# Queries and keys of two heads as one product on two levels of Strassen's algorithm, with the sums of tokens kept in DRAM

## The chip, the core and the metric

The kernel runs on one core of a Trainium2 chip. A core has five engines that run side by side and meet only at semaphores: TensorE (PE) multiplies matrices into the eight banks of PSUM, VectorE (DVE), ScalarE (ACT) and GpSimd (POOL) do elementwise work, and SyncE (SP) issues transfers to 16 DMA engines. [...] The metric is the time of one execution on the device in microseconds (us); lower is better.

## What is computed

One transformer block on 1024 tokens of width 512 in f32: layer norm, causal attention with 32 heads of width 128, its output projection added to the input, then a second layer norm and a network of three layers with weights of plus and minus one. Cut to what the change touches:

```python
q = einsum('bsd,de->bse', hidden_states, wq).reshape(B, S, H, DQ)   # DQ = 192, the first 128 are used
kv = einsum('bsd,de->bse', hidden_states, wkv)
k = kv[..., :H * DN].reshape(B, S, H, DN)
v = kv[..., H * DN:H * (DN + DV)].reshape(B, S, H, DV)
scores = einsum('bqhd,bkhd->bhqk', q[..., :DN], k) * DQ ** (-0.5)
probs = softmax(where(causal, scores, -1e30))
attn = einsum('bhqk,bkhd->bqhd', probs, v).reshape(B, S, H * DV)
return einsum('bse,ed->bsd', attn, wo)
```

## The kernel before

**Tiles and pairs.** The normalised tokens stand transposed in SBUF as `xnT` (128 partitions, 4 chunks of the width, 1024 tokens; L245). Heads are worked on in 16 pairs (`G` = 2). Each pair has 16 steps, one for each head and block of 128 queries. While a pair's scores, softmax and values run, the queries and keys of the next pair are made.

**One level of Strassen's algorithm.** A product of a 2 x 2 and a 2 x 2 arrangement of blocks takes eight block products, or seven if sums of blocks are multiplied. `products(which, g)` (L356) makes the queries (`which` = 0), keys (1) or values (2) of a pair with seven. The two halves of the width are the inner index, the two heads one outer index, the two halves of the tokens the other. The sums of tokens `T` are made once (`token_sums`, L285), the sums of weights for each pair on POOL (`weight_sums`, L307). For queries and keys, each of the seven products is two matmuls of 512 columns; for values, eight of 128. Products go into three PSUM banks, named X, Y and Z, and each `yield` ends one of the seven. X takes products 1 and 3, Y takes 2, 4 and 6, Z takes 5 and 7; a bank is read out (by ACT into `p1`, by DVE in `plus`) before the next product is accumulated into it. Pair 0 has plain products (`qk_plain`, L321).

**Scores and softmax.** `probabilities` (L513) multiplies queries and keys into `sc`, a single tile of two banks; DVE applies the mask and finds the extreme (L528), ACT takes the exponential and scales (L539, L544). `transpose_blocks` (L547) transposes 32 x 32 blocks on DVE, and `exchange` (L585) moves these blocks to where the transposed matrix has them, with 16 DMAs for each 512 queries. `attend` (L598) multiplies with the values some steps later.

**Order.** Matmuls and the transfers of `load` (L64) are pinned: they run on TensorE and SP in the order in which the program emits them. Other instructions are ordered by a scheduler. What TensorE does in a step is chosen by a planner in the loop from L700. Each step first emits the next step's scores and softmax (L750). After steps 3, 7, 11 and 15 it emits an `exchange` (L754). Then it takes products from the chain of 21 (7 for the values of this pair, 7 for the queries and 7 for the keys of the next) and parts of the output projection, up to a goal of columns (L761). The attend falls four steps after its exchange for the first 512 queries and six for the second (`ATTEND_AFTER`, L661). Weights are loaded at steps 2, 7, 12 and 15.

Of the kernel before, what the change touches and what calls it, by code (L numbers as in the profile page):

```python
# [19 lines left out]
G = 2  # L20
# [9 lines left out]
def kernel(  # L30
# [55 lines left out]
    heads = pool("heads", 4)  # L86
# [5 lines left out]
    ps_mm = pool("ps_mm", 3, space=bass.MemoryType.PSUM)  # L92

    DH = D // 2

    w_raw, w_sum, wv_sb, wo_sb = {}, {}, {}, {}
# [5 lines left out]
    def load_qk_weights(which, g, heads_of=range(G)):  # L102
        if (which, g) not in w_raw:
            w_raw[which, g] = pairs.tile(
                [P, G, NC, DN], F32, tag="wraw", name=f"w{'qk'[which]}{g}"
            )
        for i in heads_of:
            h = g * G + i
            if which == 0:
                src = wq_v[:, :, h, :DN]  # L110
            else:
                src = wkv_v[:, :, h * DN : (h + 1) * DN]
            load(w_raw[which, g][:, i, :, :], src)
# [21 lines left out]
    zeros = const.tile([P, P], F32, tag="zeros", name="zeros")  # L135
    nc.vector.memset(zeros, 0.0)
    idle = ps_sc.tile([P, S], F32, tag="sc", name="ps_idle")
    for _ in range(13):
        nc.tensor.matmul(idle[:, :P], lhsT=zeros, rhs=zeros, start=True, stop=True)  # L139
# [12 lines left out]
        fill=BIG,  # L152
# [124 lines left out]

# [13 lines left out]
    def A(which, g, i, j):  # L291
        c = slice(2 * j, 2 * j + 2)
        if which == 2:
            return wv_sb[g][:, c, i * DV : (i + 1) * DV]
        return w_raw[which, g][:, i, c, :]
# [11 lines left out]
    def weight_sums(which, g):  # L307
        w_sum[which, g] = sums_of(
            lambda i, j: A(which, g, i, j), "wsum", f"wsum{'qkv'[which]}{g}", 2
        )  # L310

    qT, kT, vs, attn = {}, {}, {}, {}

    def new_qk(which, h):
        dst = (qT, kT)[which]
        dst[h] = heads.tile(
            [P, S], F32, tag=("qT", "kT")[which], name=f"{'qk'[which]}T{h}", bufs=(4, 3)[which]
        )
        return dst[h]

    def qk_plain(between):  # L321
# [3 lines left out]
        for which, h in outs:  # L325
            new_qk(which, h)
        banks = {}
        for n_units in range(NT * 2 * G):
# [8 lines left out]
            for c in range(NC):  # L337
                matmul(
                    banks[n][:, i * P : (i + 1) * P],
                    lhsT=w_raw[which, 0][:, h, c, :],  # L340
                    rhs=xnT[:, c, t * P : (t + 1) * P],
                    start=(c == 0),
                    stop=(c == NC - 1),
                    skip_group_check=True,
                )
            if i == TPB - 1:
                keep_first(
                    nc.scalar.activation(
                        (qT, kT)[which][h][:, k * QB : (k + 1) * QB],
                        banks[n],  # L350
                        AF.Copy,
                        scale=(-scale, 1.0)[which],
                    )
                )

    def products(which, g):  # L356


        s = w_sum[which, g]
        mul = (-scale, 1.0, 1.0)[which]  # L360
        n = f"{'qkv'[which]}{g}"
        if which == 2:
            d = []
            for h in (g * G, g * G + 1):
                vs[h] = heads.tile([P, NT, DV], F32, tag="v", name=f"v{h}", bufs=3)
                d.append([vs[h][:, k * TPB : (k + 1) * TPB, :] for k in range(NQB)])
        else:
            d = [
                [t[:, k * QB : (k + 1) * QB] for k in range(NQB)]
                for t in (new_qk(which, g * G), new_qk(which, g * G + 1))  # L370
            ]

        def bank(name):
            shape = [P, TPB, DV] if which == 2 else [P, QB]
            return ps_st.tile(shape, F32, tag="st", name=f"{name}_{n}")

        def kept(name):
            shape = [P, TPB, DV] if which == 2 else [P, QB]
            return const.tile(shape, F32, tag=name, name=f"{name}_{n}")

        def product(ps, a, b, first, last):
            for c in range(2):
                start, stop = first and c == 0, last and c == 1
                if which != 2:
                    matmul(
                        ps,
                        lhsT=a[:, c, :],
                        rhs=b[:, c, :],
                        start=start,
                        stop=stop,  # L390
                        skip_group_check=True,
                    )
                    continue
# [10 lines left out]
        def plus(out, ps, other):  # L404
            if which == 0:
                nc.vector.scalar_tensor_tensor(out, ps, mul, other, ALU.mult, ALU.add)
            else:
                nc.vector.tensor_tensor(out, ps, other, ALU.add)

        X = bank("X")  # L410
        product(X, A(which, g, 0, 0), B(0, 0), True, False)
        p1 = kept("p1")
        nc.scalar.activation(p1, X, AF.Copy, scale=mul)
# [4 lines left out]
        plus(u2, Y, p1)  # L418
        yield
        product(X, A(which, g, 0, 1), B(1, 0), False, True)  # L420
        nc.scalar.activation(d[0][0], X, AF.Copy, scale=mul)
# [3 lines left out]
        plus(u3, Y, p1)  # L425
# [3 lines left out]
        plus(d[1][1], Z, u3)  # L429
        yield  # L430
        product(Y, A(which, g, 1, 1), T[3], False, True)
        plus(d[1][0], Y, p1)
        yield
        product(Z, s[3], B(1, 1), False, True)
        plus(d[0][1], Z, u2)
# [77 lines left out]
    def probabilities(h, qt):  # L513
        n = (qt + 1) * P
        sc = ps_sc.tile([P, S], F32, tag="sc", name=f"sc{h}_{qt}")
        for first in range(0, n, QB):
# [3 lines left out]
                lhsT=qT[h][:, qt * P : (qt + 1) * P],  # L520
                rhs=kT[h][:, cols],
# [10 lines left out]
            scale=1.0,  # L532
# [25 lines left out]
    def transpose_last(qt, p):  # L558
        qb, i = divmod(qt, TPB)
        if i == 0:  # L560
            spare = (heads, "qT"), (heads, "qT"), (heads, "kT"), (heads, "v")
            bufs = {"kT": 3, "v": 3}
# [3 lines left out]
            else:  # L566
                last_pT[qb] = [
                    pl.tile(
                        [P, 2, TPB, P], F32, tag=tag, name=f"pT_last{m}", bufs=bufs.get(tag)
                    )  # L570
                    for m, (pl, tag) in enumerate(spare)
                ]
        for m in range(qt // 2 + 1):
# [24 lines left out]
    def attend(h, qb, pT):  # L598
        g, j = divmod(h, G)
# [6 lines left out]
        if h == H - 1:  # L606
            ps = ps_mm.tile([P, TPB, P], F32, tag="mm", name=f"ps_av{h}_{qb}")
            for kc in range(nk):
# [7 lines left out]
                )  # L616
            nc.vector.tensor_copy(dst.rearrange("p (t i) -> p t i", t=TPB), ps)
            return
        ps = ps_mm.tile([P, NB, TPB, B32], F32, tag="mm", name=f"ps_av{h}_{qb}")
        for kc in range(nk):  # L620
# [7 lines left out]
            )  # L628
        nc.vector.tensor_copy(dst.rearrange("p (t a i) -> p a t i", a=NB, i=B32), ps)  # L629
# [3 lines left out]
    def products_of_pair(g):  # L633
        yield from products(2, g)
        if g + 1 < NG:
            yield from products(0, g + 1)
            yield from products(1, g + 1)
# [14 lines left out]


    def score_cols(qt):
        return (qt + 1) / TPB

    def value_cols(qb):
        return qb * TPB + (TPB + 1) / 2

    PRODUCT, O_PART = 2.0, 1.0  # L660
    ATTEND_AFTER = (TPB, TPB + 2)  # L661
# [35 lines left out]
    weight_sums(2, 0)  # L697
    load_qk_weights(0, 1)

    for i, (h, qt) in enumerate(steps):  # L700
# [3 lines left out]
        if s == 0:  # L704
            n_chain = 21 if g + 1 < NG else 7
# [3 lines left out]
            if g + 2 < NG:  # L709
                out_by = [max(0, (14 * (t - 2) + 12) // 13) for t in range(G * NT)]  # L710
            elif g + 2 == NG:
                out_by = [0, 0, 0, 2, 4, 6, 6, 8, 10, 12, 13, 14, 14, 14, 14, 14]
            else:
                out_by = [max(0, t - NT + 1) for t in range(G * NT)]
            done, chain_done, out_done = 0.0, 0, 0
            total = (
                2 * G * sum(score_cols(t) for t in range(NT))
                + PRODUCT * n_chain
                + o_cols * n_out
            )  # L720
            chain_end = 14 if g + 1 < NG else 6
        if s == 0:
            chain = products_of_pair(g)
            if g + 1 < NG:
                weight_sums(0, g + 1)
        if h == 2 and qt == 0:
            ffn_constants()
        if s == 2:
            if g + 1 < NG:
                load_qk_weights(1, g + 1)  # L730
# [4 lines left out]
        if s == 6 and g + 1 < NG:  # L735
            weight_sums(1, g + 1)
# [5 lines left out]
        if s == 12:  # L742
            if g + 1 < NG:
                weight_sums(2, g + 1)
            if g + 2 < NG:
                load_qk_weights(0, g + 2)
# [10 lines left out]
        late = i not in to_attend  # L757
        if not late:
            done += value_cols(to_attend[i][1])
        goal = total * (s + 1) / (G * NT)  # L760
        while True:  # L761
            want_chain = chain_done < min(n_chain, n_chain * (s + 1) / chain_end)
            want_out = out_done < min(n_out, out_by[s])
            if want_chain and (done < goal or chain_done + 2 < n_chain * (s + 1) / chain_end):
                next(chain)
                chain_done += 1
                done += PRODUCT
            elif want_out and (done < goal or out_done + 2 < out_by[s] or g + 2 == NG):
                next(o_chain)
# [4 lines left out]
            if not late:  # L774
                attend(*to_attend.pop(i))
                late = True
        if not late:
            attend(*to_attend.pop(i))
# [5 lines left out]
        if h == H - 1:  # L784
            if qt == 0:
                attend(h, 1, None)
# [31 lines left out]
    h1[1] = (part(keep, "pT0", "h1_hi1"), part(pairs, "wraw", "h1_lo1", 2))  # L818

    def network_input(t):  # L820

        k, i = divmod(t, TPB)
        pl, tag = ((heads, "kT"), (work, "p"))[k] if i < 3 or k == 1 else (heads, "v")
        xn = pl.tile([P, D], F32, tag=tag, name=f"xn_f{t}", bufs=3)
# [73 lines left out]
    attend(H - 1, 0, None)  # L898
# [12 lines left out]
    h1[0] = (part(keep, "tb0", "h1_hi0"), part(heads, "qT", "h1_lo0", 2))  # L911
# [44 lines left out]
```

## Time and profile before

Three runs took 1355.72 to 1356.49 us, median 1355.75. The profiled execution took 1356.68 us; its span from first to last instruction is 1354.9 us.

| group of instructions | count | busy us | mean ns |
|---|---|---|---|
| TensorE, scores, all widths | 768 | 290.1 | 486 |
| TensorE, probabilities by values | 744 | 250.3 | 486 |
| TensorE, first products of queries (X_q), 512 columns | 120 | 56.4 | 592 |
| DVE, sum out of PSUM for keys (u_k), 512 wide | 30 | 20.7 | 691 |
| ACT, copy out of PSUM for keys (p_k), 512 wide | 15 | 8.7 | 581 |
| POOL, sums of value weights, first of four, 256 wide | 16 | 11.7 | 728 |
| POOL, sum for the output (L457), 512 wide | 14 | 17.8 | 1269 |
| DMA, exchange of blocks, 128 KB and 64 KB | 992 | – | – |

A matmul of f32 stands in the trace as two records. Records overlap, since matmuls are pipelined, so a mean of 592 ns is the stay of one record and not its price; the price is read from the distance between starts. The DMA queue of SP moved 138.22 MB, with the 16 DMA engines busy 48.6% of the time; half the exchange's issues are of 128 KB and half of 64 KB. The granted clock of TensorE shows as 9 (90% or more) in all 40 slices.

### The profile page before, as it was taken

To read this page: it belongs to the slowest core of one execution; us is meant where nothing else is said; L and a number is where in the kernel's file an instruction comes from. 1 tells how busy PE (TensorE), PEld (TensorE's weight loads), DVE (VectorE), ACT (ScalarE), POOL (GpSimd) and SP (SyncE) were. 2 spreads that over 40 slices of the span, in tenths; PEclk is the share of its full clock that TensorE was granted. 3 is DMA by queue.
4 is the path that set the end of the run, shared out by engine and by line. 5 is a ranking of instruction groups with operands and counts; after the bars stand their busy time and mean duration, and the time that the engine had idled before them with its cause. 6 is when DMAs were issued, how large, how long until landed. Compare 5 with 4: busy or idle time off the path is not lost.

```text
span 1354.9 us, 16376 instructions
## 1 busy us (share of the span) xinstructions
PE 1346.6 (99%) x5598; PEld 873.1 (64%) x5598; DVE 806.8 (60%) x1669; ACT 500.0 (37%) x928; POOL 262.6 (19%) x324
## 2 busy tenths in 40 slices
PE   9999999999999999999999999999999999999999
PEld 9747575665757566575756657575665756657567
DVE  5455565656556565665656566565656656676574
ACT  3534333333333333343333334333333333335331
POOL 3311122211212221121222102122120212110200
PEclk9999999999999999999999999999999999999999
DMA  5356464444646444564644456464455545446301
GB/s 187 78 109 125 90 133 90 103 96 97 140 88 129 96 91 99 106 140 82 130 95 88 104 109 139 79 126 94 88 113 109 125 87 117 88 82 129 66 1 63
DMA packets 259651, 139.27 MB, mean 103 GB/s; under 512 B 18288, under 2 KB 253552, under 8 KB 259568
## 3 DMA queue, kind: packets, MB, share of 16 engines
q1 hardware_dynamic: 259568, 138.22, 48.6%
q8 instruction: 45, 0.74, 0.2%
q14 instruction: 38, 0.31, 0.1%
HBM read 38.54 MB, written 2.10 MB: 30 GB/s over the span
## 4 chain that ended last, share of the span: by engine, by line
PE 99%; DVE 1%; ACT 0%; issue 0%; ACTq 0%; DVEq 0%
PE sc L79 18%; PE ps_av L79 18%; PE ps_o L79 15%; PE Y_v L79 6%; PE Y_k L79 6%; PE Y_q L79 6%; PE Z_v L79 4%; PE X_v L79 4%; PE X_q L79 4%; PE Z_q L79 4%; PE Z_k L79 4%; PE X_k L79 4%; PE ps_qk L79 2%; PE ps_h L79 2%; PE ps_out L79 1%; PE ps_idle L139 0%
## 5 line engine op out<-in xcount | busy, mean ns | idle before, releaser
L539 ACT ACTIVATE p<-p,nmax 128x128 f32<-128x128 f32 (+7 forms) x256 | 199.0, 777 | 674.3 <-DVE nmax L528 672.3
L79 PE MATMUL sc<-kT,qT 128*128 128x512 f32 (+3 forms) x768 | 290.1, 486 | 1.4 <-DVE nmax L528 1.4
L79 PE MATMUL ps_av<-pT,v 128*128 128x512 f32 x744 | 250.3, 486 | 0.0
L528 DVE CUSTOM_DVE_ANT_0 p<-sc,mask 128x128 f32<-128x128 f32 (+7 forms) x256 | 191.3, 747 | 90.4 <-PE sc L79 90.4
L550 DVE STREAM_TRANSPOSE tb<-p 128x128 f32<-128x128 f32 (+1 forms) x248 | 187.2, 769 | 75.8 <-ACT p L544 72.2
L544 ACT ACTIVATE p<-p,rtotal 128x128 f32<-128x128 f32 (+7 forms) x256 | 197.0, 775 | 78.1 <-DVE rtotal L543 78.0
L79 PEld LDWEIGHTS ps_av<-pT,v 128*128 128x128 f32 x744 | 141.0, 190 | 127.7 <-issue 103.1
L79 PEld LDWEIGHTS sc<-kT,qT 128*128 128x128 f32 x768 | 138.7, 190 | 90.0 <-issue 77.5
L491 DVE TENSOR_TENSOR acc<-acc,ps_o 128x512 f32<-128x512 f32 x190 | 128.7, 682 | 56.0 <-PE ps_o L79 50.8
L79 PE MATMUL ps_o<-wo,attn 128*128 128x256 f32 (+1 forms) x400 | 111.3, 414 | 0.3 <-DVE attn L629 0.3
L543 DVE RECIPROCAL rtotal<-total 128x1 f32<-128x1 f32 x256 | 40.3, 158 | 113.2 <-ACT p L539 112.9
L79 PEld LDWEIGHTS ps_o<-wo,attn 128*128 128x128 f32 x400 | 72.9, 190 | 30.6 <-issue 22.3
L452 POOL TENSOR_TENSOR at<-attn,attn 128x512 f32<-128x512 f32 x14 | 17.7, 1262 | 348.3 <-DVE attn L629 348.3
L629 DVE COPY attn<-ps_av 128x512 f32<-128x512 f32 x62 | 42.2, 680 | 49.8 <-PE ps_av L79 49.8
L79 PEld LDWEIGHTS X_v<-wv,xnT 128*128 128x128 f32 x512 | 62.2, 192 | 5.1
L79 PE MATMUL X_v<-wv,xnT 128*128 128x128 f32 x512 | 62.3, 275 | 0.0
L79 PEld LDWEIGHTS ps_o<-osum,at 128*128 128x128 f32 x224 | 42.5, 190 | 22.8 <-issue 19.1
L301 POOL TENSOR_TENSOR wsumk<-wk 128x256 f32<-128x256 f32 x15 | 10.9, 726 | 235.6 <-PE Z_v L79 124.7
L79 PE MATMUL X_q<-xnT,wq 128*128 128x512 f32 x120 | 56.4, 592 | 0.0
L79 PE MATMUL X_k<-xnT,wk 128*128 128x512 f32 x120 | 56.4, 592 | 0.0
L79 PE MATMUL ps_o<-osum,at 128*128 128x256 f32 x224 | 55.0, 379 | 0.0
L539 ACT ACTIVATION_READ_ACCUMULATOR p<-p,nmax 128x1 f32 x256 | 48.1, 188 | 0.0
(177 smaller groups left out, 1648.6 us busy)
## 6 DMA issues: line engine op xcount, KB each, us to landing
pT<-tb SPq DMA_DIRECT2D x496, 128.0 KB, 3.1
pT<-tb SPq DMA_DIRECT2D x496, 64.0 KB, 2.1
wq<-in_L_attn_wq_dram SPq DMA_DIRECT2D x32, 256.0 KB, 3.3
wk<-in_L_attn_wkv_dram SPq DMA_DIRECT2D x32, 256.0 KB, 4.2
wv<-in_L_attn_wkv_dram SPq DMA_DIRECT2D x16, 512.0 KB, 4.0
wo<-in_L_attn_wo_dram SPq DMA_DIRECT2D x16, 512.0 KB, 3.7
x_in<-_attn_hidden_states_dram SPq DMA_DIRECT2D x8, 256.0 KB, 5.4
acc<-_attn_hidden_states_dram SPq DMA_DIRECT2D x8, 256.0 KB, 7.1
```

The costliest lines, as they stand in the source:

```text
L79: keep_order(nc.tensor.matmul(*args, **kw))
L301: nc.gpsimd.tensor_tensor(t[:, 0], a(1, 0), a(1, 1), ALU.add)
L452: nc.gpsimd.tensor_tensor(t0, b(0, 1), b(0, 0), ALU.subtract)
L491: nc.vector.tensor_tensor(dst, dst, ps, ALU.add)
L528: nc.vector.tensor_tensor_reduce(out=p[:, :n], in0=sc[:, :n], in1=mask[:, S - n :], scale=1.0, scalar=BIG, op0=ALU.add, op1=ALU.min, accum ...
L539: nc.scalar.activation(p[:, :n], p[:, :n], AF.Exp, bias=nmax, scale=-1.0, accum_out=total)
L543: nc.vector.reciprocal(rtotal, total)
L544: nc.scalar.activation(p[:, :n], p[:, :n], AF.Copy, scale=rtotal)
L550: nc.vector.transpose(tb[qb][:, : qt + 1, :, i, :], p[:, :n].rearrange("p (c b k) -> p c b k", b=NB, k=B32))
L629: nc.vector.tensor_copy(dst.rearrange("p (t a i) -> p a t i", a=NB, i=B32), ps)
```

## The change

Queries and keys of both heads of a pair become one product on two levels. The outer level has as its inner index the halves of the width, and as outer indices queries or keys and the halves of the tokens. Each of its seven products is again done with seven, over the halves within the half width, the two heads, and quarters of the tokens. That makes 49 matmuls of 256 columns where there were 2 x 7 x 2 = 28 of 512. Two outer products that go to the same outputs share a bank, side by side, so the 49 are worked through in four groups: three with two outer products (seven units of two matmuls each) and a last one with a single outer product (seven units of one matmul).

- The weights of a pair stand in one tile `w_qk` of seven slots; POOL makes the outer sums in place (`qk_weight_sums`) and the inner sums group by group (`qk_block_sums`).
- The inner sums of tokens are the same for every pair. They are made once in pair 0 (`make_t`, steps 1, 2, 4 and 5), stored in DRAM, and read back for each group of each pair into four single buffers t0 to t3 (`load_t`). A load for the next group is emitted right after the product that used the buffer.
- Outputs are accumulated in SBUF: groups 0 and 1 write their parts, POOL combines halves of them, groups 2 and 3 add theirs (`add_to` on POOL, `plus` on DVE).
- The planner: products carry a first and a due step. Groups 0 to 2 of the next pair run in steps 7 to 14, group 3 in steps 0 to 2 of that pair beside the value products. Attends are emitted in parts of two matmul chunks and interleaved with products. The output projection's due steps and the weights' loading steps move.
- The scale is applied in DVE's first softmax operation and the mask's sign is turned. Queries and keys of a head share a tile. There are 10 warm-up matmuls instead of 13.

```diff
+    HB = QB // 2
+    GROUPS = (
+        ((0, B(0, 0)), (5, T[1])),
+        ((2, T[2]), (4, T[0])),
+        ((1, B(1, 0)), (3, T[3])),
+        ((6, B(1, 1)),),
+    )
...
+    def make_t(grp):
+
+        bs = [b for _, b in GROUPS[grp]]
+        t = [new_t(n, f"new{grp}") for n in range(4)]
+        for m, b in enumerate(bs):
+            r = [x[:, m] for x in t]
+            nc.gpsimd.tensor_tensor(r[0], right(b, 0, 1), right(b, 0, 0), ALU.subtract)
+            nc.gpsimd.tensor_tensor(r[1], right(b, 1, 1), r[0], ALU.subtract)
+            nc.gpsimd.tensor_tensor(r[3], right(b, 1, 0), r[1], ALU.subtract)
+            nc.gpsimd.tensor_tensor(r[2], right(b, 1, 1), right(b, 0, 1), ALU.subtract)
+        for n in range(4):
+            t_kept[grp, n] = dram.tile(
+                [P, len(bs), HB], F32, tag=f"t{grp}{n}", name=f"t_kept{grp}{n}"
+            )
+            load(t_kept[grp, n], t[n][:, : len(bs)])
...
+    def load_t(grp, n, g):
+        t_now[n] = new_t(n, f"{grp}_{g}")
+        nm = len(GROUPS[grp])
+        load(t_now[n][:, :nm], t_kept[grp, n])
...
+        def product(ps, a, b, first, last):
+            for m in range(nm):
+                matmul(
+                    ps[:, m],
+                    lhsT=a[:, m, :],
+                    rhs=right(bs[m], *b) if isinstance(b, tuple) else t_now[b][:, m],
...
+            if not isinstance(b, tuple) and (nxt or g + 1 < NG):
+                load_t(nxt, b, g + (nxt == 0))
...
+        X = bank("X")
+        product(X, a00, (0, 0), True, False)
...
+        product(Y, s1, 1, True, False)
+        u2 = kept("u2")
+        plus(u2, Y, p1)
+        add_to(u2, 0, 1)
+        yield
+        product(X, a01, (1, 0), False, True)
...
+        product(Y, s2, 2, False, False)
+        u3 = kept("u3")
+        plus(u3, Y, p1)
+        add_to(p1, 1, 0)
+        add_to(u3, 1, 1)
+        yield
...
+        product(Z, s0, 0, True, False)
...
+        product(Y, a11, 3, False, True)
...
+        product(Z, s3, (1, 1), False, True)
...
+        for to, add in {0: ((1, 0),), 1: ((2, 1), (1, 3), (3, 2))}.get(grp, ()):
+            for h in hs:
+                d = qk[h].rearrange("p w (m n) -> p (w m) n", m=2)
+                nc.gpsimd.tensor_tensor(d[:, to], d[:, to], d[:, add], ALU.add)
+        if grp < 2:
+            qk_block_sums(grp + 2, g)
...
+        chain = [[2.0, 0, n, values] for n in range(7)]
+        if g > 0:
+            last = qk_products(3, g)
+            for at, step in ((0, 0), (2, 0), (3, 0), (5, 1), (6, 1), (8, 2), (9, 2)):
+                chain.insert(at, [0.5, 0, step, last])
         if g + 1 < NG:
...
+            first, n = NT - 1, 0
+            for grp in range(3):
+                gen = qk_products(grp, g + 1)
+                for _ in range(7):
+                    n += 1
+                    chain.append([1.0, first, first + (n * NT - 1) // 21, gen])
...
+        if g == 0 and s in (1, 2, 4, 5):
+            make_t((1, 2, 4, 5).index(s))
+            if s == 5:
+                for n in range(4):
+                    load_t(0, n, 1)
+        if g + 1 < NG:
+            if s == 3:
+                qk_weight_sums()
+            if s in (4, 5):
+                qk_block_sums(s - 4, g + 1)
...
         if qt % TPB == TPB - 1 and h < H - 1:
             qb = qt // TPB
             to_attend[i + ATTEND_AFTER[qb]] = (h, qb, exchange(h, qb))
...
+        if s == G * NT - 1 and g + 2 < NG:
+            for which in range(2):
+                load_qk_weights(which, g + 2)
...
+            if chain and chain[0][1] <= s and (
+                chain[0][2] <= s or done < goal and chain[0][2] <= s + 1
+            ):
+                cols, _, _, gen = chain.pop(0)
+                mine.append(gen)
+                done += cols
```

## The prediction

> **What bounds the kernel now.** I read the busy table first, then the chain of waits, then the chain's pieces in order of time through one pair of heads, then the timelines of the DMA queue and of POOL.
>
> ```profile
> PE 1346.6 (99%) x5598; PEld 873.1 (64%) x5598; DVE 806.8 (60%) x1669; ACT 500.0 (37%) x928; POOL 262.6 (19%) x324
> PE 99%; DVE 1%; ACT 0%; issue 0%; ACTq 0%; DVEq 0%
> ```
>
> TensorE has no idle time worth naming, and the chain that ended last is TensorE from end to end. Removed TensorE work is therefore worth its full time, and an added wait costs its full time: nothing absorbs it. The pieces (start, length, what) give the price of each unit:
>
> ```profile
> 600.39 1.72 PE X_q L79 x4
> 602.11 0.86 PE ps_o L79 x4
> 612.65 1.72 PE sc L79 x4
> 661.91 1.78 PE X_v L79 x16
> ```
>
> A matmul of f32 is two records. A 512-column matmul takes 0.86 us (1.72 for two), a 256-column one 0.432 us (0.86 for two ps_o), so half the columns cost half the time. One pair lasts 680.02 - 600.39 = 79.6 us (from one X_q to the next).
>
> **TensorE work removed.** Before: 14 products x 1.717 = 24.04 us per pair for queries and keys. After: 49 matmuls of 256 columns x 0.4325 = 21.19 us. Saved 2.85 us x 15 pairs = **-42.7 us**. The weight loads (190 ns, two per matmul) stay beside the matmuls, as they do for ps_o.
>
> **Work added on the other engines, per pair.** DVE: sums out of PSUM grow from 10 of 512 columns to 16 of 512 (0.69 us each, as u_k) and 6 of 256 (about 0.42, as the 256-wide copy of pT_last): +6.7 us on some 50. ACT: +0.9 us. POOL: its 512-element sum takes 1.27 us (the at row), its 256-element sum 0.73. Weight sums 4 x 1.27, block sums 12 x 0.73 and 4 x 0.42 (an estimate from those two), values 4 x 0.73, additions into u2, p1, u3 3 x 1.27 and 3 x 0.73, combinations of halves 8 x 1.27: 34.6 us where 8.8 us stood; with the sums for the output POOL works 43 of 77 us. None becomes the bound; TensorE's 77 us hide them where a product has time until its bank is wanted. That time shrinks: the next product into the same bank comes one product later, which was 1.72 us and is now 0.865, while one DVE sum takes 0.69 plus the hand-over. Following the planner's loop for a middle pair, four places have such neighbours (steps 8, 10, 12, 14), and the first scores of the next pair follow the last product directly. Each costs nothing if DVE is free and about 1 us if a 1 us softmax operation stands ahead. Step 8 is hidden by the wait found below; for the rest I take 0.7 us a pair, 14 pairs: **+10 us** (ends 0 and 42, at 3 us a pair, if POOL's additions into group 2 are late for step 14). The mask's sign, the scale moved into DVE's first operation and the scale dropped from ACT change no count: 0. Three fewer warm-up matmuls: 0, since the first rows are ready at about 5.8 us and the clock is not up before 7 us anyway.
>
> **The loads of token sums.** Each pair adds 16 loads (12 of 256 KB, 4 of 128 KB). Their bytes are no trouble (DMA 49% busy); their place in SP's queue is. Each buffer t0 to t3 is single, so a load can go out only after the product that read it, and SP issues in program order. Group 0's products start in step 7, and in step 7 the 16 DMAs of `exchange` are put into the queue before any product. So the loads of group 1 stand behind this:
>
> ```profile
> 619.78 11.10 SPq L66 DMA_DIRECT2D pT<-tb  x16
> wq<-in_L_attn_wq_dram SPq DMA_DIRECT2D x32, 256.0 KB, 3.3
> ```
>
> The exchange starts at 619.78, when the transpose for the 1024-column scores (piece at 612.65) is done: 7.1 us after these scores start. It holds SP for 11.1 us. A 256 KB load then lands 3.3 us after issue, taken from the weights, the nearest row (the output's 256 KB take 2.0, its ends 2.0 to 4.2). So the first load of group 1 lands 7.1 + 11.1 + 3.3 = 21.5 us after those scores start. TensorE wants it as group 1's second product, and counted by the planner there lie between: scores 1.72, last value product 1.78, scores 0.22, group 0's seven products 6.06, half an attend 2.16, scores 0.43, one output unit 0.86, scores 0.65, group 1's first product 0.86: 14.7 us. **TensorE waits 6.8 us in each of 14 pairs: +95 us** (ends 5.5 and 8). Behind the waiting matmul, in pinned order, stands everything TensorE does: the next scores, so DVE and ACT too. The other three loads of group 1 go out right after and land in time; group 2's are emitted before step 11's exchange, group 3's and the next group 0's have more than 10 us to spare.
>
> Here a rule speaks for the change. The Trainium skill ("DMA: Bandwidth & Descriptors", section "Issuing engines are not separate DMA queues") says that the time to initiate a DMA is usually small beside the DMA itself. By it the load would go out when its product ends and land some 5 us early: 0 us. The row says 11.1 us of issuing against 3.3 us of landing, so I go by the row.
>
> **The clock.** A rule that speaks against it: "TensorE: Matmul & The Clock Gate" (section "HAM oscillation — how this bites in real kernels") warns of idle gaps over about 3.4 us, after which the array runs at half clock until it has been busy for such a window again. The trace shows both edges:
>
> ```profile
> 1.08 5.92 PE ps_idle L139 x26
> 1352.00:1356.00 4.00, 0.00 (x0) 0.00 (x0) 0.26 (x1) 0.00 (x0) 0.00 (x0) 0.90 0.24 83
> ```
>
> The first 26 records, 128 columns each, take 5.92 us, 228 ns each; the X_v piece above has 16 of the same size in 1.78 us, 111 ns: the clock starts at half. At the end, TensorE stops at 1351.7, and the granted clock of the last four microseconds is 0.90, which is half clock for the last 0.8 us (an estimate, if it fell to half): it fell some 3.5 us after the last matmul. A wait of 6.8 us is longer. By the page's window, restarting costs half of 3.4 us, 1.7; by the row, half of 5.9 us, 2.9. I take 2.3 us for 15 pairs: **+34 us** (ends 0 and 44). Were the trace's 1.00 through the body to hold, this term is 0.
>
> **The first pair.** The halved token sums are made once on POOL, which is not early:
>
> ```profile
> 39.90 2.35 POOL L289 TENSOR_TENSOR xnT<-xnT 128x1024 f32<-128x1024 f32 x1 [0.87 <-PE ps_qk L79]
> ```
>
> POOL is free at 42.2. Then come 8, 8, 8 and 4 sums of 256 (20.4 us), the weight sums 5.1, two sets of block sums 5.8, waits of about 1 us for stores into DRAM to release the single buffers, then the store and load back, two landings of 2 to 3 us: group 0's first sum is there at about 76. TensorE reaches that product at 40.3 + 21 = 61.4 (the planner puts only scores and value products before it). Wait 14.6 us, then 3.5 us at group 1's load: **+18 us**, once (ends 8 and 28). What is late next is that exchange, already counted.
>
> **Sum**, against the profiled execution's 1356.7 us (span 1354.9 plus 1.8 around it): -42.7 + 10 + 95 + 34 + 18 = +114, so 1471; the median of the runs is 0.9 lower, so **1470 us**.
>
> **Rivals.**
> *The loads come in time (faster).* One mechanism: SP gets the loads out before or between the exchange. For it: SP's issues fill only some 53 of 77 us (64 exchange DMAs 43, weights and sums 10), and all loads but one have room. It decides below a lateness of 0.2 us per pair for the wait to be gone. Then 1355.8 - 42.7 + 18 = 1331 us. Against it: the queue's order in the trace (exchange, weights, exchange) is the program's order.
> *The wait is there but the clock holds.* For it: a clock of 1.00 in all body slices. Against: the drop at the end. 1470 - 34 = 1436.
> *Handing over instead of the queue.* Loads in time, but each neighbouring product waits for DVE, some 5 places of 0.75 us in 15 pairs, 56 us: 1331 + 56 = 1387. Against it: DVE has a quarter of its time free.
> *The wait plus POOL's chain.* Group 2's sums hold step 14 for 3 us a pair: 1470 + 45 = 1515. For it: seven to eight POOL operations of 1.27 us follow group 1's end. Against: one attend of 5.6 us lies between.
> *It does not do what it says:* would show as matmul records other than 98 per pair of 256 columns; the code gives no reason.
>
> **Chances.** Forecast 57% (own range 1445 to 1500), clock holds 20%, wait plus POOL 8%, loads in time 7%, handing over 6%, close to no change 2%. The range 1405 to 1515 covers the first two, and about half the third. A measurement of this kernel tells about 0.2% from no change; faster by more 7%, within it 2%, slower 91%.
>
> **What would show it.** Right: in each pair one TensorE wait of 6 to 8 us before the second product of group 1, with a load of t1 as releaser and 16 exchange DMAs ahead of it on SP; a granted clock under 1.0 in the body; TensorE busy below 95%; a wait of about 15 us near 61 us. The queries' and keys' records should fall to some 21.2 us per pair. Wrong: the queue handing out that load before 44 us into the pair, or waits that name DVE or POOL.

## The result and the profile after

The changed kernel takes 1513.39 us (median of four runs, 1512.83 to 1515.19) beside 1356.12 us of the kernel before: **1.116 times as long** [1.1142, 1.1181], 157 us slower. The profiled execution has a span of 1510.7 us. From its page, the busy table, the granted clock in 40 slices and the chain of waits:

```profile
PE 1364.3 (90%) x6222; PEld 1010.1 (67%) x6222; DVE 897.1 (59%) x1849; ACT 511.5 (34%) x958; POOL 663.9 (44%) x742
PEclk9889999999999999999999999999999999999999
PE 55%; DVE 11%; SPq 11%; POOL 9%; ACT 6%; DMA 4%; issue 4%; POOLq 0%; ACTq 0%; DVEq 0%
```

TensorE was 99% busy and is 90% busy. SP's queue and POOL, which the chain before did not contain, now carry 20% of it. The slices of the clock still show 9 nearly everywhere; the mean granted clock is 0.959, so the loss is in stretches too short for slices of 38 us. TensorE's waits, by releaser (total us, times, longest us):

```profile
PE Y_qk L79 <- DMA t<-t_kept: 113.8, 16, 13.5
PE Z_qk L79 <- DVE qk L517: 18.7, 15, 4.1
```

The first row is the loads of token sums: 13.5 and 5.3 us in the first pair, and 95.0 us in the 14 pairs that follow, 6.8 to 7.4 us in each but the last, mean 7.0 (3.7 in the last). TensorE's timeline in a middle pair shows where (start, length, then in brackets the idle time before it and who ended it), and the chain's pieces of the same pair show why (start, length, what):

```profile
613.84 0.60 PE L79 MATMUL X_qk<-T,w_qk 128*128 128x256 f32 x2
621.23 2.04 PE L79 MATMUL Y_qk<-t,asum 128*128 128x256 f32 x4 [6.79 <-DMA t<-t_kept]
...
652.21 0.70 PE L79 MATMUL Z_qk<-xnT,asum 128*128 128x256 f32 x2 [1.09 <-DVE qk L517]
```

```profile
606.67 0.58 SPq L66
...
617.01 0.74 SPq L66
617.75 0.05 issue
617.85 3.24 DMA t<-t_kept
621.09 0.14 issue
621.23 2.04 PE Y_qk L79 x4
```

From 606.67 to 617.75 SP issues the 16 DMAs of the exchange of step 7, 11.08 us. Only then does the load go out; it lands 3.24 us later, and group 1's second product starts. The load's issue did not wait for its data or its buffer; it waited for its turn.

The rows by stretches of the same pair give length, then busy time of PE, PEld, DVE, ACT and POOL, then the granted clock, the DMA share and GB/s:

```profile
605.00:621.00 16.00, 9.44 (x40) 6.82 (x38) 8.21 (x17) 4.48 (x11) 7.11 (x9) 0.95 0.79 157
621.00:625.00 4.00, 3.77 (x9) 3.08 (x10) 0.69 (x1) 0.00 (x0) 0.00 (x0) 0.50 0.59 189
625.00:629.00 4.00, 4.00 (x15) 3.02 (x15) 2.08 (x4) 0.58 (x1) 0.00 (x0) 0.84 0.09 34
```

After the wait the clock is 0.50 for four microseconds and 0.84 in the next four: half clock until about 626.3, which is 5.05 us of work at half pace, 2.5 us lost.

Pairs, from one X_v to the next, took 79.6 us before and take 88.5 to 89.0. TensorE's work alone would be 79.6 - 2.85 = 76.8, and the records of a changed pair, each at the distance that its width takes to the next one in the kernel before (0.216 us for a record of 256 columns), add up to that. The 11.9 us above it are the starts that come later than this. They are 7.0 for the load, 2.5 for the clock (2.2 by experiment 3), 1.6 before products into Z_qk, of which 1.1 show as the wait above, and 0.8 before products into Y_qk and X_qk. Most of these last delays are 0.1 to 0.3 us long and show as no idle time, since records overlap: group 0's sixth product, into Y_qk, starts at 610.01 and its seventh, into Z_qk, at 610.98, 0.97 us later where 0.865 is the price.

### The profile page after: what moved, and what is told of

Its sections match the earlier page's. It is cut to its first block, busy times and chain, and to the rows that moved or that the text cites. A ratio compares the mean times of both kernels' runs of the same rounds, so it can differ in the third digit from the quotient of the medians.

```text
span 1510.7 us, 18967 instructions
## 1 busy us (share of the span) xinstructions
PE 1364.3 (90%) x6222; PEld 1010.1 (67%) x6222; DVE 897.1 (59%) x1849; ACT 511.5 (34%) x958; POOL 663.9 (44%) x742
## 4 chain that ended last, share of the span: by engine, by line
PE 55%; DVE 11%; SPq 11%; POOL 9%; ACT 6%; DMA 4%; issue 4%; POOLq 0%; ACTq 0%; DVEq 0%
SPq L66 11%; PE ps_o L79 10%; PE sc L79 9%; PE ps_av L79 9%; POOL qk L560 8%; PE Y_v L79 6%; PE X_v L79 4%; PE Z_v L79 4%; DMA t<-t_kept 4%; PE Y_qk L79 3%; ACT p L671 3%; DVE p L655 3%; DVE tb L677 3%; PE X_qk L79 2%; ACT p L666 2%
## 5 line engine op out<-in xcount | busy, mean ns | idle before, releaser
L79 PE MATMUL sc<-qk 128*128 128x512 f32 (+3 forms) x768 | 291.1, 488 | 5.5 <-DVE nmax L655 5.5
L560 POOL TENSOR_TENSOR qk<-qk 128x512 f32<-128x512 f32 x120 | 153.2, 1278 | 296.2 <-DVE qk L517 290.3
L79 PEld LDWEIGHTS sc<-qk 128*128 128x128 f32 x768 | 139.6, 192 | 79.6 <-issue 65.1
L79 PE MATMUL Y_qk<-t,asum 128*128 128x256 f32 x210 | 71.5, 467 | 113.8 <-DMA t<-t_kept 113.8
L517 DVE TENSOR_TENSOR u_qk<-Y_qk,p_qk 128x512 f32<-128x512 f32 (+1 forms) x120 | 74.0, 617 | 120.8 <-PE Y_qk L79 119.8
L79 PE MATMUL Y_qk<-t,w_qk 128*128 128x256 f32 x420 | 114.4, 389 | 1.1 <-POOL asum L470 0.8
L79 PEld LDWEIGHTS Y_qk<-t,w_qk 128*128 128x128 f32 x420 | 75.3, 190 | 34.1 <-issue 13.0
L517 DVE TENSOR_TENSOR qk<-Z_qk,u_qk 128x512 f32<-128x512 f32 (+1 forms) x120 | 74.9, 624 | 26.3 <-POOL u_qk L522 15.1
L79 PE MATMUL X_qk<-xnT,w_qk 128*128 128x256 f32 x240 | 79.6, 416 | 0.0
L522 POOL TENSOR_TENSOR u_qk<-u_qk,qk 128x512 f32<-128x512 f32 (+1 forms) x60 | 61.0, 1016 | 32.2 <-DVE u_qk L517 32.2
```

Of the source, the lines that this page charges most:

```text
L79: keep_order(nc.tensor.matmul(*args, **kw))
L522: nc.gpsimd.tensor_tensor(x, x, dst(i, k), ALU.add)
L560: nc.gpsimd.tensor_tensor(d[:, to], d[:, to], d[:, add], ALU.add)
```

## The experiments

Every time below is a median beside runs of the kernel before on the same chip.

**1. The load's turn: the exchange after step 8's products.** The exchange of step 7 is emitted one step later, so the loads of group 1 stand ahead of it.

```diff
-            to_attend[i + ATTEND_AFTER[qb]] = (h, qb, exchange(h, qb))
+            if s == NT - 1 and g + 1 < NG:
+                waiting = (i + ATTEND_AFTER[qb], h, qb)
+            else:
+                to_attend[i + ATTEND_AFTER[qb]] = (h, qb, exchange(h, qb))
...
+        if s == NT and g + 1 < NG:
+            at, eh, eqb = waiting
+            to_attend[at] = (eh, eqb, exchange(eh, eqb))
```

> The 16 DMAs of step 7's exchange are put into the queue after step 8's products instead of before step 7's, so that the four loads of group 1 go out ahead of them. Theory (place in the queue): the wait of 6.8 us before group 1's second product goes in 14 pairs (95 us), that in the first pair of 5.3 us as well, and with them the half clock after each (about 2.5 us, 37 us): 1513 - 137 = about 1376 us. Rival (the loads themselves are slow, some 52 MB more through DRAM): the loads land as late as before, 1500 us or more. Rival (the clock does not matter): 1513 - 100 = about 1413 us.

Measured: 1430.32 us, ratio 1.0547 [1.053, 1.0563]. The forecast of 1376 is missed. The wait at group 1 is gone from the body but for 0.9 and 1.0 us in two pairs, and 83 of the 157 us with it; but the pairs last 81.4 to 84.3 us, not 77 to 79. A new wait stands at group 2's fourth product. TensorE's and VectorE's timelines:

```profile
596.93 1.10 PE L79 MATMUL Y_qk<-t,w_qk 128*128 128x256 f32 x4 [3.19 <-issue]
```

```profile
594.11 0.16 DVE L670 RECIPROCAL rtotal<-total 128x1 f32<-128x1 f32 x1 [1.09 <-ACT p L666]
594.49 1.77 DVE L677 STREAM_TRANSPOSE tb<-p 128x640 f32<-128x640 f32 x2 [0.21 <-DMA pT<-tb]
596.18 0.65 DVE L517 TENSOR_TENSOR u_qk<-Y_qk,p_qk 128x512 f32<-128x512 f32 x1
```

TensorE needs bank Y, and bank Y is free when u_qk has been read out of it at 596.8. This sum stood ready since 592.9, when the product before had ended, but on VectorE the scheduler has put a reciprocal, which waits for ScalarE, and two transposes, which wait for the exchange (DMA pT<-tb), ahead of it. In the changed kernel u_qk comes right after the mask of these scores, in the pair shown above:

```profile
637.83 0.69 DVE L517 TENSOR_TENSOR u_qk<-Y_qk,p_qk 128x512 f32<-128x512 f32 x1
```

Moving the exchange had changed VectorE's order.

**2. The same with half of the exchange.** Eight of its DMAs after step 7's, eight after step 8's products.

```diff
+            if s == NT - 1 and g + 1 < NG:
+                pT, part_of = exchange(h, qb, later=True)
...
+        if s in (NT - 1, NT) and g + 1 < NG:
+            part_of(range(NB // 2) if s == NT - 1 else range(NB // 2, NB))
```

> Step 7's exchange is put into the queue in two halves, 8 DMAs after step 7's products and 8 after step 8's, so that the loads of group 1 go out between them and the exchange ends about 1 us later than before the split. Theory (place in the queue, and the run with the whole exchange moved stayed at 1430 because DVE's transposes, which wait for the late exchange, now stand ahead of a sum that TensorE needs): the wait before group 1's second product goes and no wait of 3 us takes its place: 1513 - 100 (waits) - 37 (clock) = about 1376 us. Rival (any load issued in that stretch is late, since the 16 DMA engines are over 90% busy): waits of 3 us or more remain at group 1, 1430 us or more.

Measured: 1434.86 us, ratio 1.0589 [1.0561, 1.0617]: a miss, with the same wait of 3.2 to 3.5 us at the same product in 13 pairs, and of 6.5 us in the last.

**3. The clock: TensorE kept busy while it waits.** Group 1 gets 14 products of a weight of zeros, added into X while the load is under way. They add 14 x 0.4325 = 6.06 us of work to a wait of 7.0 us, so what changes is the clock.

```diff
+        if grp == 1:
+            for n in range(14):
+                matmul(X[:, n % 2], lhsT=mask[:, :P],
+                       rhs=right(bs[n % 2], 0, 0),
+                       start=False, stop=False, skip_group_check=True)
```

> 14 matmuls of 256 columns with zero weights (6.1 us) are added into bank X between group 1's first product and the read-out of X, so that TensorE is busy where it waited; the loads and the wait for them stay. Theory (each long wait also costs about 2.5 us at half clock): the waits shrink below 1 us, the clock stays at 1.00, and 15 x 2.5 = 37 us go: about 1476 us, though 85 us of work are added. Rival (the half clock hides nothing and costs nothing, or the matmuls add to the wait): 1513 us or more; 1598 us if the added work comes on top.

Measured: 1485.94 us, ratio 1.0957 [1.0941, 1.0973]. TensorE's waits, first row:

```profile
PE Y_qk L79 <- DMA t<-t_kept: 29.4, 14, 13.3
```

In pairs 2 to 14 the wait is now 0.8 to 2.0 us, mean 1.24, the mean clock 0.991 (1.00 over 600 to 690), and these pairs last 86.8 us on average, not 88.7. The run is 27.5 us shorter, where the theory had 37 and the rival none. Zeros and wait together are 6.06 + 1.24 = 7.3 us, 0.3 longer than the wait was, so the half clock was worth 1.9 + 0.3 = 2.2 us a pair; the wait itself is still paid for with zeros.

**4. Handing over: no combinations.** The six operations of POOL that combine halves after group 1 are left out, so the queries and keys lack these parts.

```diff
-        for to, add in {0: ((1, 0),), 1: ((2, 1), (1, 3), (3, 2))}.get(grp, ()):
+        for to, add in {0: ((1, 0),)}.get(grp, ()):
```

> Leaves out the six combinations of halves after group 1, so queries and keys lack these parts. Theory: DVE no longer stands behind POOL, the waits before group 2's last product (18.7 us in all) go, and up to 1 us more of short waits in each pair: 1480 to 1495 us. Rival (POOL's sums are hidden, the hand-over of banks between neighbouring products is what costs): 1510 to 1513 us.

Measured: 1497.05 us, ratio 1.104 [1.1023, 1.1056], 16.3 us less and 2 us above the forecast range. The Z_qk row of the waits:

```profile
PE Z_qk L79 <- DVE qk L517: 2.8, 14, 0.2
```

It fell from 18.7 to 2.8 us, nearly all of those 16 us. In the changed kernel the operations stand like this on POOL and on VectorE, of the pair shown above:

```profile
632.20 3.98 POOL L560 TENSOR_TENSOR qk<-qk 128x512 f32<-128x512 f32 x3 [14.91 <-DVE qk L517]
636.14 0.45 POOL L469 TENSOR_TENSOR asum<-w_qk 128x128 f32<-128x128 f32 x1
...
637.92 3.96 POOL L560 TENSOR_TENSOR qk<-qk 128x512 f32<-128x512 f32 x3
641.84 1.27 POOL L522 TENSOR_TENSOR u_qk<-u_qk,qk 128x512 f32<-128x512 f32 x1
```

```profile
641.91 0.69 DVE L517 TENSOR_TENSOR qk<-X_qk,qk 128x512 f32<-128x512 f32 x1 [3.40 <-POOL qk L560]
```

One head's three combinations, then block sums for the next groups, then the other head's three. VectorE, which adds group 2 to the head that comes last, stands idle for 3.40 us, and what is behind it is late up to the wait at 652.21. The chain's pieces lead from the one to the other; at "..." stand VectorE's and ScalarE's softmax operations:

```profile
641.91 0.69 DVE qk L517
...
651.55 0.61 DVE qk L517
652.17 0.04 issue
652.21 1.13 PE Z_qk L79 x4
```

**5. The same work in a better order.** Emitting the first head's combinations first, by exchanging the two loops, changed nothing in any engine's order: the scheduler chose the same, and that run repeats the changed kernel.

> POOL's six combinations of halves after group 1 are emitted head by head instead of operation by operation, so that the three of the first head are done 2.5 us earlier. Theory (DVE stands 3.4 us behind these sums, which makes TensorE wait 1.2 us before group 2's last product): DVE's stand shrinks to about 1 us and TensorE's wait goes: 1513 - 15 = about 1498 us. Rival (that wait comes from elsewhere): 1513 us.

Measured: 1514.35 us, ratio 1.1165 [1.1146, 1.1183]. With the order pinned it does change:

```diff
-        for to, add in {0: ((1, 0),), 1: ((2, 1), (1, 3), (3, 2))}.get(grp, ()):
-            for h in hs:
-                d = qk[h].rearrange("p w (m n) -> p (w m) n", m=2)
-                nc.gpsimd.tensor_tensor(d[:, to], d[:, to], d[:, add], ALU.add)
+        for h in hs:
+            d = qk[h].rearrange("p w (m n) -> p (w m) n", m=2)
+            for to, add in {0: ((1, 0),), 1: ((2, 1), (1, 3), (3, 2))}.get(grp, ()):
+                keep_order(nc.gpsimd.tensor_tensor(d[:, to], d[:, to], d[:, add], ALU.add))
```

> The combinations of halves on POOL are pinned in program order, first head first (without the pin the scheduler takes the second head and sums of weights first). Theory: the first head's three are done before the product that adds to them is read out, DVE's stand of 3.4 us goes, and with it TensorE's wait of 1.1 us before group 2's last product: 1513 - 15 = about 1498 us, as with the combinations left out (1497). Rival (POOL is late as a whole, whatever the order): 1513 us.

Measured: 1500.48 us, ratio 1.1076 [1.1045, 1.1107]; the Z_qk wait is 6.8 us. No work was taken away, and 13 of the 16 us went: most of it was order, not POOL's amount of work.

**6. Both together, and the first pair.** Half of the exchange later and the pinned combinations; then, in a further run, the first pair's token sums half on VectorE, in the order of groups 1, 2, 3, 0, with group 0 kept in SBUF for the first use and the first attend two steps later.

> Both together. Theory (the two causes are separate): 1376 - 16 = about 1360 us. If they overlap: about 1376 us.

> Both, and in the first pair half of the token sums are made on DVE, group 0's sums are made last and used from SBUF instead of being read back, and the first attend comes two steps later. Theory (13.5 us of wait plus 2.5 us of half clock, once): 1360 - 12 = about 1348 us, 0.6% below the kernel before. Rival (POOL's 40 us in the first pair are the bound): 1358 us or more.

Measured: 1433.63 us (ratio 1.0572 [1.0556, 1.0587]) and 1431.17 us (1.0559 [1.054, 1.0578]). Both missed by over 70 us: the wait of 3.2 us at group 2's fourth product stays in 13 pairs of each, and is 6.2 us in the last. All four versions that moved the exchange ran into VectorE's order.

**7. The loads on another queue.** The exchange stays where the change has it; only the engine that issues the loads is another.

```diff
-        load(t_now[n][:, :nm], t_kept[grp, n])
+        nc.scalar.dma_start(t_now[n][:, :nm], t_kept[grp, n])
```

> The changed kernel, with nothing but the loads of token sums issued from ACT's queue instead of SP's: same loads, same bytes, same single buffers, the exchange untouched. Theory (place in SP's queue): the loads of group 1 go out when their product has been read, the waits of 6.8 us and the half clock behind them go: 1513 - 100 - 37 = about 1376 us, with the 1.1 us before group 2's last product still there. Rival (the bytes through DRAM, or the 16 DMA engines at over 90% in that stretch): 1430 us or more.

Measured: **1374.43 us**, ratio 1.0129 [1.0112, 1.0146], 2 us from the forecast. One line took 139 of the 157 us away. TensorE's waits, and the DMA issues from the page (KB each, median us to landing):

```profile
PE Z_qk L79 <- DVE qk L517: 17.0, 15, 3.9
PE Y_qk L79 <- DMA t<-t_kept: 15.0, 1, 15.0
```

```profile
t<-t_kept ACTq DMA_DIRECT2D x180, 256.0 KB, 4.2
```

One wait for a load is left, in the first pair. The load does not land sooner after its issue (4.2 us, 3.9 on SP's queue); it is issued sooner. The scheduler answered this edit too with another order on VectorE, ScalarE and POOL; what went is nevertheless the load's wait, 113.8 to 15.0 us, and the half clock behind it. The clock is 0.992, and the steady pairs last 79.0 us, 2.2 above TensorE's work. By the starts of records, 1.5 of these 2.2 us stand before products into Z_qk, the rest before those into Y_qk and X_qk.

**8. The queue, the order and the first pair together.** Loads on ScalarE's queue and pinned combinations, with three forms of the first pair: that of experiment 6; that form with groups 1 and 3 built in buffers that stand empty then; and all sums on POOL in the order 0, 1, 2, 3, groups 1 to 3 in such buffers.

```diff
+        spare = ("at0", "at1", "at3", "attn10")
+        t = [
+            new_t(n, f"new{grp}")
+            if grp == 0
+            else const.tile([P, 2, HB], F32, tag=spare[n], name=f"t{n}_new{grp}")
+            for n in range(4)
+        ]
```

> The loads on ACT's queue, the combinations pinned first head first, and the first pair as in the run with half of its token sums on DVE. Theory (the three causes add up): 1376 - 16 - 16 = about 1344 us, 0.9% below the kernel before; this is what the saved TensorE work leaves when its waits are gone. Rival (ACT, which now waits for TensorE in order, delays the softmax): 1356 us or more.

> As the run with the loads on ACT's queue, pinned combinations and half of the first pair's token sums on DVE, but groups 1 and 3 of these sums go to buffers that the first pair does not use otherwise, so that no sum waits for a store that stands behind the exchange. Theory (the first pair was not helped before because DVE's sums waited there for a store, 7.7 us in which the softmax stood still): the first pair falls from 81.6 us to about 68, and the whole from 1363 to about 1350 us, 0.4% below the kernel before. Rival (POOL's and DVE's sums themselves fill the first pair): 1360 us or more.

> Loads on ScalarE's queue and pinned combinations as in e9_act_pin_first; the first pair's token sums are made by POOL alone, in the order of groups 0, 1, 2, 3; group 0 stays in SBUF for the first pair, groups 1 to 3 are built in buffers that nothing else uses yet, and the first attention starts two steps later. Theory (what is left of the loss to the kernel before lies in the first pair, whose sums stand in the way of other work on VectorE and of stores behind the exchange): the first pair falls from 81.6 us to 62 to 66, the later pairs stay at 78.2 us, and the time is about 1345 us, 0.8% below the kernel before. Rival (the sums, some 40 us of POOL's work, hold the first pair wherever they stand): the first pair stays at 75 us or more and the time is 1356 us or more.

Measured: 1363.44 us (1.005 [1.0035, 1.0065]), 1361.98 us (1.0036 [1.0022, 1.0049]) and **1352.52 us (0.997 [0.9961, 0.998])**. The first two missed their forecasts by 19 and 12 us, the third lies between its theory and its rival. It is 0.3% below the kernel before, clear of the noise. Steady pairs are 78.2 us in all three, 1.4 less than before. First pairs are 81.6, 75.5 and 71.4 us, where before it was 63.8. In the second the first pair also starts 4.6 us later than before. The waits of the third, first rows:

```profile
PE ps_av L79 <- DMA pT<-tb: 5.7, 1, 5.7
PE sc L79 <- DVE nmax L665: 5.5, 4, 2.2
PE Z_qk L79 <- DVE qk L525: 5.1, 14, 2.4
```

The first row is in the first pair, before an attend. SP's timeline there:

```profile
60.58 9.88 SPq L66 DMA_DIRECT2D t_kept<-t_new  x8
70.97 0.38 SPq L66 DMA_DIRECT2D wv<-in_L_attn_wkv_dram  x1
71.45 28.30 SPq L66 DMA_DIRECT2D pT<-tb  x32
```

The stores of the sums into DRAM hold SP from 60.58 to 70.46, not by their issue (0.32 us each) but because each waits its turn until POOL has made its sum. The exchange that the attend needs stands behind them: the transposes whose blocks it moves ended at 64.83, and it starts at 71.45. This is the fault of the changed kernel with the parts exchanged. But its 16 DMAs then also take until 88.2 to go out, 16.8 us instead of 11.1, and the DMA share over this stretch is 1.02. How much of the wait of 5.7 us belongs to each was not tried. From the starts of the X_v, the 4.3 us by which this span is shorter than the one before are: start 1.1 earlier, first pair +7.6, 13 steady pairs -18.0, the last interval +3.4, the rest +3.8 (among it group 3 of the last pair, 7 x 0.4325 = 3.0 us, which now falls there). The arithmetic saved is real, but of 42.7 us some 4 arrive.

## Why the prediction was right, and where its sum was off

- **The direction, the place and the mechanism were right.** The wait stands before group 1's second product, behind the 16 DMAs of step 7's exchange, with a token load as releaser. The time itself, 1513, lies above the prediction's own range of 1445 to 1500 and 2 us inside the wider one that ends at 1515. Forecast were 11.1 us of issuing, 3.3 of landing and 6.8 of waiting in 14 pairs, 95 us; the trace has 11.08, 3.24, 7.0 on average and 95.0 (the last pair's is shorter). The row was the right choice against the rule on issue time: experiment 7 moved only the issuer in the program, and the time fell by 139 us. That the loads come in time (1331) is therefore what happens only when they have a queue of their own, and even then it gave 1374.
- **The clock** was forecast at 2.3 us a pair, 34 us. Keeping TensorE busy through the wait took 27.5 us away, 2.2 a pair; by the stretches it is 2.5. So the wait does drop the clock, and the rival of 1436 falls. The edge of 3.4 us of idle time, by which the prediction went, is too long: waits of 3.2 us dropped the clock too (last section).
- **TensorE's work**: 2.85 us a pair saved. In the best version the steady pair shows 1.4 less than before, and by the starts of its records 1.4 us of delays stand in it, half before Z_qk and half before Y_qk and X_qk, so the saving is there in full.
- **The first pair** was forecast at +18, as waits of 14.6 and 3.5; they are 13.5 and 5.3, 18.8 together. As an interval, with its half clock and short delays, it grew by 23.0 us (86.8 for 63.8).
- **The mis-sized term is the handing over**: 0.7 us a pair, +10 us. The trace has 2.4 a pair (11.9 - 7.0 - 2.5), some 36 us in 15 pairs, and 2.2 with the load's wait removed alone. It has two parts. Pinning the combinations takes 0.8 a pair away (79.0 to 78.2): this is POOL's chain, put at nothing in the sum. What is left, 1.4 a pair, stands in the best version in seven places between neighbouring products, 0.06 to 0.5 us each, and where the trace names who ended one it is mostly VectorE's sum out of the bank. This is the term that the prediction had, at half its size, and no run removed it.
- **Why POOL's chain was put aside.** The prediction named it as an upper end, "at 3 us a pair, if POOL's additions into group 2 are late for step 14", and held against it that an attend of 5.6 us lies between. The attend is there, at 641.92, but the lateness passes it by on another engine. In the pair shown, what is waited for is not the additions but the combinations before them: VectorE, standing behind them until 641.91, brings the softmax and the sum that frees bank Z late as well, and TensorE waits at 652.21 all the same. Experiments 4 and 5 are the evidence: 16 us with the combinations after group 1 left out, 13 us with only their order changed. That the rival with this chain, 1515, came within 2 us is in part luck: it has 45 us for POOL's chain, and the runs 13 to 16; the neighbouring products, the clock and the first pair make up the rest.

## What to carry to other kernels

A load that is small in bytes can be late by its place: count the DMAs that one engine issues ahead of it, times their measured issue time, and put what TensorE waits for on a queue without a long block in it; here that took more away than moving the block. When TensorE has no idle time, follow each in-place chain on a slower engine through the order that the scheduler gives it, and pin that order; moving one DMA can reorder an engine that was not touched. A slower engine can also hold TensorE up by way of a third one, so work that lies between on TensorE does not hide it. A saving of 3% of the work in a full engine is lost to a few waits of one microsecond.

## What the chip showed that was not expected

**SP's issue time does not follow size.** The 16 DMAs of 128 KB of the exchange shown take 0.58 to 0.74 us each, 11.08 together; the 16 of 64 KB that follow at 631.58 take 10.76 together, while a weight load of 512 KB at 651.56 takes 0.38. On ScalarE's queue one load of token sums is a row of 0.33 us in most places, about what it is on SP (median 0.38): what ScalarE's queue changes is what stands ahead. ScalarE's own work then waits behind loads at times (3.46 us before a softmax operation at 601.27 in experiment 7), but no wait of TensorE for ScalarE came with it.

**The clock changes on a grid of 3.41 us.** With half of the exchange later and the combinations pinned, waits of 3.2 to 3.5 us cost different amounts: pairs of 83.1, 84.4 and 81.4 us have a mean clock of 0.98, 0.96 and 1.00. These are the rows of their three waits, divided where the clock can change, in the columns above:

```profile
429.55:432.96 3.41, 0.22 (x2) 0.23 (x2) 2.81 (x5) 1.29 (x3) 3.33 (x3) 1.00 0.54 106
432.96:436.38 3.42, 3.42 (x9) 2.71 (x9) 1.00 (x3) 0.00 (x0) 3.34 (x4) 0.50 0.60 139
511.47:514.88 3.41, 1.20 (x6) 0.72 (x4) 1.75 (x5) 1.97 (x3) 3.33 (x3) 1.00 0.52 102
514.88:521.71 6.83, 5.56 (x11) 3.85 (x12) 3.14 (x5) 0.00 (x0) 6.35 (x6) 0.50 0.48 106
678.73:682.14 3.41, 1.43 (x7) 0.92 (x5) 2.11 (x5) 1.96 (x3) 3.33 (x3) 1.00 0.42 84
682.14:685.56 3.42, 2.21 (x9) 1.82 (x10) 2.60 (x5) 0.00 (x0) 3.26 (x4) 1.00 0.54 103
```

Within a run, all changes of the clock lie whole multiples of 3.41 us apart. In the first stretch TensorE is idle for 3.2 of 3.41 us, and half clock follows for one stretch, 1.7 us lost. In the second wait it is idle for 2.2 us of a stretch, and half clock follows for two, with 5.56 us of work in them: 2.8 us lost. The third wait is as long as the first, but falls on two stretches with 2.0 and 1.2 us of idle time, and the clock holds. In all 14 traces, leaving out the first 8 us, every stretch at full clock with more than 2.0 us of idle time was followed by half clock, and none with less than 1.9. So a wait at this edge costs 0 to 3 us on top of itself by where it falls on the grid. The changed kernel's wait of 6.8 us has a whole stretch in it (616.03 to 619.44), and half clock follows for two, 619.44 to 626.27: 1.8 us of them are still waiting, 5.04 are work.
